# Graph layer with scattered messages: layer 2 one step after layer 1, the last group's layer 1 moved forward, and two half-size node blocks at the end

## The chip, the cores and the metric

The kernel runs on one core of a Trainium2 chip. The metric is device time in microseconds; for a set of runs the median is given, with the lowest and highest.

## What is computed

There are 12500 nodes with 64 features and 200000 edges, sorted by destination. Each edge takes its two nodes and its own 64 features, makes a message, and adds it to its destination. Then each node gets a small network on its sum, and a normalization. Cut to what matters:

```python
nodes = node_state[edges].reshape(num_edges, -1)            # rows src and dst, 128 features
gates = ssp(edge_state @ We1 + be1) @ We2 + be2             # ssp(x) = softplus(x) - log 2
gates = gates * (1.0 - sigmoid(5.0 * (edges_distance - 3.5)))
h = ssp(nodes @ Wn1 + bn1) @ Wn2 + bn2
messages = h * gates
message_sum = zeros_like(node_state).at[edges[:, 1]].add(messages)
new_state = node_state + (ssp(message_sum @ Ws1 + bs1) @ Ws2 + bs2)
out = layernorm(x + new_state)
```

All data is float32.

## The kernel before

**Groups.** The edges are cut into NG = 391 groups of 512, each in two halves of 256. Since they are sorted, the destinations of a half lie in a window of W = 42 nodes from a base that the kernel finds itself. The destination half of the first node layer is done once for all nodes at the start, into a table in memory (line 412); a group loads the 42 rows of its windows from it (`load`, line 143, with the edge features) and picks among them with a one-hot matrix.

**What one group does.** `gather` (line 135) fetches the 512 source rows by four indirect transfers from POOL, line 138. `onehot` (DVE, line 154) writes the window's one-hot columns beside them. `transposes` (PE, line 159) turn both into PSUM tile `tx`; `xcopy` (ACT, line 164) copies that to SBUF. `layer1_edge` (PE, lines 169 and 171) and `layer1_node` (PE, line 176) fill `z`. `exps` and `logs` (ACT, lines 183 and 186) and `softplus` (DVE, line 190) make `s`. `layer2_edge` (PE, lines 195 and 198) and `layer2_node` (PE, line 203) fill `gh`. `hcut` and `message` (DVE, lines 208 and 212) multiply the parts. `scatter` (PE, line 217) sums messages by window, and `window` (DVE, line 226) adds the windows into `sums`, which holds all nodes.

**Order.** The order is written out by hand in the loop of lines 435 to 468. Each engine works through its own instructions in that order. In step i, PE does layer 2's edge part of group i - 1, layer 1 of group i + 1, the transposes of i + 2, layer 2's node part of i - 1, and the scatter of i - 2. ACT does xcopy of i + 2 and then exp and log of i + 1. DVE does hcut and message of i - 1, window of i - 2, onehot of i + 4 and softplus of i + 1. SP issues the loads of group i + 5, POOL the gather of group i + 19; the first 20 gathers stand ahead of the loop. There are 24 gather buffers, two each of `z`, `gh`, `xT`, `u`, three of `s`, one of `tx` and `sc`.

**Node blocks.** A block is NB = 512 nodes in order; there are 25, the last with 212. Once every edge into a block is summed, `node_block` (line 228) does it in five parts, one per step: `hidden` (PE, line 247) and `clamp`; `logs` (ACT, lines 259 and 260) and `ssp` (DVE, line 263); `layer2` (PE, lines 268 and 271) and `center`; `square` and `variance`; `root` and `store`. PE's share goes between layer1_edge and layer1_node, into a free part of `z`; the rest goes at the end of the step. `clamp` loads y and `store` writes the result, both through SP's queue. `block_steps` (line 70) sets the step at which a block is put on the list, from the expected share of edges below its last node plus MARGIN = 3 steps. A guard (`least`, line 583, compared at line 373) makes the kernel redo what lies outside a window, or too early, in a second pass from line 477. Blocks that are left when the loop ends are done one part of each in turn, from line 469.

## Time and profile before

| what | value |
|---|---|
| median of 3 runs | 2621.21 us (2603.5 to 2627.03) |
| the profiled execution | 2002.57 us |
| its span, first to last instruction | 2000.7 us |
| PE busy | 1883.2 us, 94%, 11375 matmuls |
| POOL busy | 1487.4 us, 74% |
| DVE busy | 1119.8 us, 56% |
| ACT busy | 921.7 us, 46% |
| moved by DMA | 142.85 MB, 71 GB/s |

The profile is of one execution. Busy time is the time in which an engine ran an instruction; a share is of the span. A line number (L138) is that of the kernel above. A group of instructions is named by line, engine, operation and tiles (output <- input), with its count, busy time and the mean of one in ns. A wait is put down to the instruction or transfer that came last before the waiting one could start. PEclk is the granted clock of PE as a share of the full one. The timeline lists start and duration in us; an x4 after a row means that four such instructions were merged.

### The profile page before, as it was taken

The numbers are of one execution on the slowest core, as the hardware profiler recorded it, in microseconds if no ns is written. First come the engines' busy times: TensorE is split into PE (matmuls) and PEld (weight loads), VectorE is DVE, ScalarE is ACT, GpSimd is POOL, SyncE is SP. The second block draws the span as 40 slices with busy tenths as digits, with TensorE's granted clock in tenths as the row PEclk, the third lists the DMA queues.
The fourth block names the chain that finished last, engine by engine and source line by source line (L and its number), as shares of the span: only waits on it lengthen the run. The fifth ranks groups of instructions, "written<-read, shape, count | busy, mean of one in ns | idle before, by whom it ended". The sixth has DMA issues, their size and how long they took to land.

```text
span 2000.7 us, 37114 instructions
## 1 busy us (share of the span) xinstructions
PE 1883.2 (94%) x11375; PEld 1516.5 (76%) x11375; DVE 1119.8 (56%) x2762; ACT 921.7 (46%) x1315; POOL 1487.4 (74%) x1568
## 2 busy tenths in 40 slices
PE   4999999999999999999999999999999999999997
PEld 4788888888778777777877777777777777777775
DVE  4455555556546546554654655555465565665555
ACT  1355455454445444443544444444444454444443
POOL 7777777777777777777777777777777777777772
PEclk9999999999989999998999999999899999999997
DMA  8422222222222222222222222222222222222220
GB/s 235 137 79 66 66 68 67 67 69 63 69 62 62 68 61 68 65 65 58 72 57 75 64 58 72 71 64 61 58 71 71 67 67 68 64 67 71 71 71 22
DMA packets 168270, 142.85 MB, mean 71 GB/s; under 512 B 43599, under 2 KB 140027, under 8 KB 168066
## 3 DMA queue, kind: packets, MB, share of 16 engines
q1 hardware_dynamic: 116650, 87.54, 15.0%
q0 software_dynamic: 50048, 51.35, 11.5%
q10 hardware_dynamic: 1368, 1.51, 0.3%
q8 instruction: 95, 1.56, 0.3%
q14 instruction: 109, 0.89, 0.1%
HBM read 130.60 MB, written 9.63 MB: 70 GB/s over the span
## 4 chain that ended last, share of the span: by engine, by line
PE 59%; DMA 16%; POOL 12%; issue 7%; DVE 4%; DVEq 1%; ACT 0%; POOLq 0%; SPq 0%; ACTq 0%
DMA xg<-in_x,src_i 15%; POOL xg L138 12%; PE gh L203 11%; PE z L176 10%; PE gh L198 8%; PE z L171 8%; PE tx L159 6%; PE sc L217 6%; PE gh L195 4%; PE z L169 3%; PE z L412 2%; DVE s L190 1%; PE z L271 1%; PE z L247 1%; DVE h L208 1%
## 5 line engine op out<-in xcount | busy, mean ns | idle before, releaser
L138 POOL DMA_INDIRECT xg<-in_x,src_i x1564 | 1487.2, 951 | 479.1 <-issue 323.0
L164 ACT COPY xT<-tx 106x512 f32<-106x512 f32 x391 | 229.2, 586 | 982.4 <-PE tx L159 982.4
L208 DVE TENSOR_TENSOR h<-gh,cut 128x256 f32<-128x256 f32 x391 | 165.8, 424 | 586.6 <-PE gh L203 568.8
L176 PE MATMUL z<-xT,wns 106*128 106x256 f32 x1564 | 414.3, 387 | 0.1
L203 PE MATMUL gh<-consts,s 128*128 128x64 f32 x3128 | 396.2, 270 | 0.0
L203 PEld LDWEIGHTS gh<-consts,s 128*128 128x128 f32 x3128 | 391.4, 196 | 0.1
L190 DVE SCALAR_TENSOR_TENSOR s<-u,z 128x768 f32<-128x768 f32 x391 | 373.2, 955 | 23.5 <-PE z L176 8.1
L186 ACT ACTIVATE u<-u,one 128x768 f32<-128x768 f32 x391 | 365.7, 935 | 12.6
L176 PEld LDWEIGHTS z<-xT,wns 106*128 106x128 f32 x1564 | 301.9, 194 | 44.5 <-issue 0.8
L159 PE MATMUL tx<-consts,xg 128*106 128x128 f32 x1564 | 274.6, 282 | 52.5 <-DMA xg<-in_x,src_i 46.9
L183 ACT ACTIVATE u<-z 128x768 f32<-128x768 f32 x391 | 319.1, 816 | 1.4 <-PE z L176 1.4
L159 PEld LDWEIGHTS tx<-consts,xg 128*106 128x106 f32 x1564 | 196.4, 133 | 137.2 <-DMA xg<-in_x,src_i 86.2
L198 PE MATMUL gh<-consts,s 128*128 128x128 f32 x1564 | 280.8, 302 | 0.0
L171 PE MATMUL z<-eT,consts 128*128 128x256 f32 x782 | 278.0, 438 | 0.5 <-DMA eT<-in_eT 0.5
L198 PEld LDWEIGHTS gh<-consts,s 128*128 128x128 f32 x1564 | 205.7, 191 | 89.2 <-DVE h L208 81.3
L226 DVE TENSOR_TENSOR sums<-sums,sc 64x42 f32 x782 | 153.7, 197 | 185.9 <-issue 148.0
L217 PE MATMUL sc<-xg,msg 128*128 128x84 f32 x1564 | 246.4, 280 | 1.3 <-DVE sums L226 1.2
L217 PEld LDWEIGHTS sc<-xg,msg 128*128 128x128 f32 x1564 | 207.4, 193 | 1.5 <-issue 1.4
L212 DVE TENSOR_TENSOR msg<-gh,h 128x256 f32<-128x256 f32 x391 | 165.9, 424 | 13.4
L171 PEld LDWEIGHTS z<-eT,consts 128*128 128x128 f32 x782 | 118.1, 190 | 48.3 <-issue 1.6
L195 PE MATMUL gh<-row,ones 3*128 3x512 bf16 x391 | 151.1, 386 | 0.0
L154 DVE TENSOR_TENSOR xg<-consts,rel 128x168 f32<-128x168 f32 x391 | 130.6, 335 | 14.7 <-issue 2.8
(73 smaller groups left out, 562.9 us busy)
## 6 DMA issues: line engine op xcount, KB each, us to landing
eT<-in_eT SPq DMA_DIRECT2D x391, 128.0 KB
xg<-in_x,src_i POOLq DMA_INDIRECT x1564
wns<-table SPq DMA_DIRECT2D x782, 21.0 KB
table<-tb SPq DMA_DIRECT2D x14, 448.0 KB
sums<-in_xT SPq DMA_DIRECT2D x7, 455.0 KB
y<-in_x SPq DMA_DIRECT2D x24, 128.0 KB
out<-y SPq DMA_DIRECT2D x24, 128.0 KB
dst_h<-in_dst_h SPq DMA_DIRECT2D x1, 896.0 KB
```

The lines of the kernel that those rows point to most:

```text
L138: nc.gpsimd.indirect_dma_start(out=xg[:, k, :D], out_offset=None, in_=x, in_offset=bass.IndirectOffsetOnAxis(ap=src_i[:, g, k : k + 1], ax ...
L159: nc.tensor.transpose(tx[:, k, :], xgs[g][:, k, :DW], ident)
L164: nc.scalar.copy(xT, xTs[g])
L171: nc.tensor.matmul(zs[g][:, 0, :HE], we1.rearrange("a h d -> a (h d)"), eTs[g], start=False, stop=True, skip_group_check=True)
L176: nc.tensor.matmul(zn, wns[:, g % REST, h, :], xTs[g][:, h], start=True, stop=True, skip_group_check=True)
L183: nc.scalar.activation(us[g], z_of(g), AF.Exp)
L186: nc.scalar.activation(us[g], us[g], AF.Ln, bias=one)
L190: nc.vector.scalar_tensor_tensor(ss[g].rearrange("p i t e -> p (i t e)"), us[g], BIG, z_of(g), OP.min, OP.max)
L195: nc.tensor.matmul(gh, ones3[:, :P], row3.rearrange("q i k d -> q (i k d)"), start=True, stop=False, skip_group_check=True)
L198: nc.tensor.matmul(v[:, 0, t], ss[g][:, 0, t, :], we2, start=False, stop=False, skip_group_check=True)
L203: nc.tensor.matmul(ghs[g][:, 1, 2 * t + h, :], ss[g][:, 1 + h, t, :], wn2, start=False, stop=h == 1 and t == 1, skip_group_check=True)
L217: nc.tensor.matmul(sc, msgs[g][:, 2 * t : 2 * t + 2, :].rearrange("p h f -> p (h f)"), xgs[g][:, 2 * t : 2 * t + 2, D:DW], start=t == 0, s ...
```

## The change

The steps run from -2 to 391 and not from -4 to 392, and layer 2 of group i, not i - 1, is done in step i, the scatter of group i - 1, not i - 2. PE's order in a step is now layer 1 of i + 1, transposes of i + 2, layer 2 of i, scatter of i - 1. On ACT, exp and log of i + 1 precede xcopy of i + 2; on DVE, softplus of i + 1 precedes hcut. In step 388 the last group's layer 1 is placed among layer 2 of group 388, and its exp, log and softplus are done in two pieces, the edge part and the node part. Three loads and two onehots stand ahead of the loop.

The node blocks are now 26: 212 nodes, 23 of 512, and two of 256. The step of each is the expected share plus five standard deviations of the count of edges below its end. By that rule they are put on the list at steps 53, 96, 125 and so on to 384 and 388, and the last one after the loop; before, at steps 83, 115, 141 to 383, 391 and 394, the last two after the loop. From step 388 on a block's part uses a `z` tile of its own and stands at the end of the step. `center` and `store` have one DVE instruction less each, and `clamp` makes both its results from PSUM.

```diff
--- before.py
+++ after.py
@@ -60,16 +60,30 @@
 K = 4
 AHEAD = 20
 LOADS = 5
-MARGIN = 3
+SPREADS = 5
 CUTOFF = 5.0
 EPS = 1e-5
 LN2 = 0.6931471805599453
 BIG = 30.0
+def node_blocks(N):
+
+    rest = N - NB
+    first = rest % NB
+    assert rest > 0 and first % 2 == 0 and first <= HE
+    sizes = ([first] if first else []) + [NB] * (rest // NB) + [HE, HE]
+    return [(sum(sizes[:i]), n) for i, n in enumerate(sizes)]
+
+
 def block_steps(N, NG):
-    return [ceil(NG * sqrt(min(1.0, (b + 1) * NB / N))) + MARGIN for b in range(-(-N // NB))]
+    steps = []
+    for at, n in node_blocks(N):
+        share = sqrt(min(1.0, (at + n) / N))
+        spread = sqrt(share * (1.0 - share) / (NG * GE))
+        steps.append(ceil(NG * (share + SPREADS * spread)))
+    return steps
 @with_exitstack
@@ -178,16 +192,21 @@
     def z_of(g):
         return zs[g].rearrange("p b e -> p (b e)")[:, : 3 * HE]
-    def exps(g):
-        us[g] = work.tile([P, 3 * HE], F32, name="u")
-        nc.scalar.activation(us[g], z_of(g), AF.Exp)
-
-    def logs(g):
-        nc.scalar.activation(us[g], us[g], AF.Ln, bias=one)
-
-    def softplus(g):
-        ss[g] = work.tile([P, 3, 2, P], F32, name="s", bufs=3)
-        nc.vector.scalar_tensor_tensor(ss[g].rearrange("p i t e -> p (i t e)"), us[g], BIG, z_of(g), OP.min, OP.max)
+    every, edge, node = slice(0, 3 * HE), slice(0, HE), slice(HE, 3 * HE)
+
+    def exps(g, part=every):
+        if part.start == 0:
+            us[g] = work.tile([P, 3 * HE], F32, name="u")
+        nc.scalar.activation(us[g][:, part], z_of(g)[:, part], AF.Exp)
+
+    def logs(g, part=every):
+        nc.scalar.activation(us[g][:, part], us[g][:, part], AF.Ln, bias=one)
+
+    def softplus(g, part=every):
+        if part.start == 0:
+            ss[g] = work.tile([P, 3, 2, P], F32, name="s", bufs=3)
+        nc.vector.scalar_tensor_tensor(ss[g].rearrange("p i t e -> p (i t e)")[:, part], us[g][:, part], BIG,
+                                       z_of(g)[:, part], OP.min, OP.max)
     def layer2_edge(g):
         gh = gh_tile()
@@ -225,15 +244,13 @@
             part = sums[h * D : (h + 1) * D, bass.ds(base, W)]
             nc.vector.tensor_add(part, part, scs[g][h * D : (h + 1) * D, h * W : (h + 1) * W])
-    def node_block(b, pool):
-
-
-        left = N - b * NB
-        nq = min(2, -(-left // HE))
-        p = min(P, left // 2)
-        assert left >= NB or (nq == 1 and left % 2 == 0)
+    def node_block(first, n, pool):
+
+
+        nq = -(-n // HE)
+        p = min(P, n // 2)
         t = {}
-        rows = slice(b * NB, b * NB + nq * p * 2)
+        rows = slice(first, first + n)
         def tile3(name):
             return pool.tile([P, 2, 2, D], F32, name=name, bufs=2)[:p, :nq]
@@ -243,17 +260,17 @@
         def hidden(z):
             t["z"] = z[:, 1, HE:]
-            for q in range(2):
+            for q in range(nq):
                 nc.tensor.matmul(t["z"], ws1[:, q].rearrange("f o d -> f (o d)"),
-                                 sums[:, b * NB + q * HE : b * NB + (q + 1) * HE], start=q == 0, stop=q == 1,
+                                 sums[:, first + q * HE : first + (q + 1) * HE], start=q == 0, stop=q == nq - 1,
                                  skip_group_check=True)
         def clamp():
             t["y"] = tile3("y")
             nc.sync.dma_start(t["y"], x[rows, :].rearrange("(q p k) d -> p q k d", q=nq, k=2))
             t["l"], t["zb"] = (pool.tile([P, HE], F32, name=name, bufs=2) for name in ("l_s", "zb"))
+            nc.vector.tensor_scalar(t["l"], t["z"], packed["bs1"], BIG, OP.add, OP.min)
             nc.vector.tensor_scalar(t["zb"], t["z"], packed["bs1"], None, OP.add)
-            nc.vector.tensor_scalar(t["l"], t["zb"], BIG, None, OP.min)
         def logs():
             nc.scalar.activation(t["l"], t["l"], AF.Exp)
@@ -275,8 +292,7 @@
             nc.vector.scalar_tensor_tensor(t["y"], t["y"], 2.0, t["u"][:, :nq], OP.mult, OP.add)
             mean = small("mean")
             nc.vector.tensor_reduce(mean, t["y"], AX.X, OP.add)
-            nc.vector.tensor_scalar(mean, mean, 1.0 / D, None, OP.mult)
-            nc.vector.tensor_sub(t["y"], t["y"], mean.to_broadcast([p, nq, 2, D]))
+            nc.vector.scalar_tensor_tensor(t["y"], mean.to_broadcast([p, nq, 2, D]), -1.0 / D, t["y"], OP.mult, OP.add)
         def square():
             t["y2"] = tile3("y2")
@@ -296,9 +312,8 @@
             v, r = t["v"], t["r"]
             nc.vector.tensor_mul(v, v, r)
-            nc.vector.tensor_mul(v, v, r)
-            nc.vector.tensor_scalar(v, v, -0.5, 1.5, OP.mult, OP.add)
-            nc.vector.tensor_mul(r, r, v)
+            nc.vector.scalar_tensor_tensor(v, v, -0.5, r, OP.mult, OP.mult)
+            nc.vector.scalar_tensor_tensor(r, v, 1.5, r, OP.add, OP.mult)
             nc.vector.tensor_mul(t["y"], t["y"], r.to_broadcast([p, nq, 2, D]))
             nc.sync.dma_start(out[rows, :].rearrange("(q p k) d -> p q k d", q=nq, k=2), t["y"])
@@ -430,43 +445,69 @@
         with tc.tile_pool(name="finish", bufs=1) as finish:
-            steps = block_steps(N, NG)
+            blocks = list(zip(node_blocks(N), block_steps(N, NG)))
+            last = NG - 1
             todo = []
-            for i in range(-4, NG + 2):
-                def at(f, g, *more):
-                    if 0 <= g < NG:
-                        f(g, *more)
-                part = todo.pop(0) if todo and i + 1 < NG else None
-                if i == -4:
-                    for g in range(LOADS - 4):
-                        load(g)
+
+            def at(f, g, *more):
+                if 0 <= g < NG:
+                    f(g, *more)
+
+            for g in range(LOADS - 2):
+                load(g)
+            for g in range(2):
+                onehot(g)
+            for i in range(-2, NG + 1):
+                part = todo.pop(0) if todo else None
                 at(load, i + LOADS)
                 if i > 0:
                     at(gather, i + AHEAD - 1)
-                at(layer2_edge, i - 1)
-                at(layer1_edge, i + 1)
-                if part and part[0]:
-                    part[0](zs[i + 1])
-                at(layer1_node, i + 1, 0)
-                at(layer1_node, i + 1, 1)
+                ending = i + 2 >= last
+                if i < last - 1:
+                    at(layer1_edge, i + 1)
+                    if part and part[0] and not ending:
+                        part[0](zs[i + 1])
+                    at(layer1_node, i + 1, 0)
+                    at(layer1_node, i + 1, 1)
                 at(transposes, i + 2)
-                at(layer2_node, i - 1, 0)
-                at(layer2_node, i - 1, 1)
-                at(scatter, i - 2)
-                at(xcopy, i + 2)
-                at(exps, i + 1)
-                at(logs, i + 1)
-                at(hcut, i - 1)
-                at(message, i - 1)
-                at(window, i - 2)
+                if i + 2 == last:
+                    exps(last - 1)
+                    xcopy(last)
+                    layer1_edge(last)
+                at(layer2_edge, i)
+                if i + 2 == last:
+                    layer1_node(last, 0)
+                    layer1_node(last, 1)
+                at(layer2_node, i, 0)
+                at(layer2_node, i, 1)
+                at(scatter, i - 1)
+                if i + 2 == last:
+                    logs(last - 1)
+                    for some in (edge, node):
+                        exps(last, some)
+                        logs(last, some)
+                elif i + 1 < last:
+                    at(exps, i + 1)
+                    at(logs, i + 1)
+                    at(xcopy, i + 2)
+                if i + 1 < last:
+                    at(softplus, i + 1)
+                at(hcut, i)
+                at(message, i)
+                at(window, i - 1)
                 at(onehot, i + 4)
-                at(softplus, i + 1)
+                if i + 2 == last:
+                    softplus(last, edge)
+                    softplus(last, node)
                 if part:
-                    part[1]()
-                for b, step in enumerate(steps):
-                    if step == i:
-                        todo += node_block(b, finish)
-            for parts in zip_longest(todo, *[node_block(b, finish) for b, step in enumerate(steps) if step > NG + 1]):
+                    if ending:
+                        node_part(part)
+                    else:
+                        part[1]()
+                for block, step in blocks:
+                    if step == i and i < last:
+                        todo += node_block(*block, finish)
+            for parts in zip_longest(todo, *[node_block(*block, finish) for block, step in blocks if step >= last]):
                 for part in parts:
                     if part:
                         node_part(part)
...
-        for b in range(NBL):
-            for part in node_block(b, o):
+        for block in node_blocks(N):
+            for part in node_block(*block, o):
                 node_part(part)
...
-    for b, step in enumerate(steps):
-        least[2 * (step - 1) : 2 * NG] = (b + 1) * NB
+    for (at, n), step in zip(node_blocks(N), steps):
+        least[2 * step : 2 * NG] = at + n
```

## The prediction

> **What bounds the kernel now.** I read the page first, then the instructions of the gather's line, the table of waits, engine busy time in windows, and last the timeline of a middle step, of a step with a node block, and of the end.
>
> The page gives PE 94% busy and POOL 74%, which points at PE. The instructions of line 138 and the windows say otherwise.
>
> ```profile
> L138 POOL DMA_INDIRECT xg<-in_x,src_i x1564: 940/945/2280, 3.3 to 1965.7; - x196
> 200.00:300.00 100.00, 100.00 (x639) 82.68 (x637) 57.35 (x136) 50.49 (x69) 75.76 (x80) 1.00 0.26 67
> 1000.00:1200.00 200.00, 189.98 (x1147) 152.44 (x1146) 112.83 (x282) 93.42 (x135) 151.31 (x159) 0.97 0.25 63
> 1800.00:1950.00 150.00, 141.67 (x871) 112.92 (x871) 86.96 (x222) 70.95 (x105) 113.43 (x121) 1.00 0.27 72
> ```
>
> In the windows the columns are length, then busy time (count) of PE, weight loads, DVE, ACT, POOL, then the clock. POOL issues 80 gathers in every 100 us from start to end: (1965.7 - 3.3) / 1563 = 1.255 us each, 5.0 us per group of four. Its "idle" 0.30 us after each one never shrinks, so POOL has no room. PE is full at 200 us and no longer at 1000 us. The starts of line 169 in the timeline are 4.41 us apart where PE is not held up; so PE, which starts at 74 us with 15 groups gathered, catches up near 525 us, and from there has 5.0 - 4.41 = 0.59 us of room per step. The waits agree:
>
> ```profile
> PEld tx L159 <- DMA xg<-in_x,src_i: 86.2, 155, 1.7
> PE tx L159 <- DMA xg<-in_x,src_i: 46.9, 99, 1.4
> PE z L271 <- DVE l_s L263: 24.8, 24, 1.1
> ```
>
> The first two are PE standing at the transposes until the gather has landed. The third is another wait: a node block's second layer (line 271) stands for DVE's `ssp`, 1.03 us each time. The timeline of such a step, and a full-clock row of an ordinary step:
>
> ```profile
> 1000.53 1.03 PE L176 MATMUL z<-xT,wns 106*128 106x256 f32 x4
> ...
> 1957.28 0.42 DVE L263 SCALAR_TENSOR_TENSOR l_s<-zb,l_s 128x256 f32<-128x256 f32 x1
> 1957.75 0.80 PE L271 MATMUL z<-consts,l_s 128*128 128x128 f32 x4 [1.03 <-DVE l_s L263]
> 1958.35 1.92 PE L176 MATMUL z<-xT,wns 106*128 106x256 f32 x4
> ```
>
> After the wait the same four matmuls take 1.92 in place of 1.03 us: the clock has fallen to half. That step lasts 8.05 us; without the fall, 6.4. The end:
>
> ```profile
> 1965.74 0.94 POOL L138 DMA_INDIRECT xg<-in_x,src_i  x1 [0.30 <-issue]
> 1969.66 0.60 PE L159 MATMUL tx<-consts,xg 128*106 128x128 f32 x4
> 1982.72 0.20 DVE L226 TENSOR_TENSOR sums<-sums,sc 64x42 f32 x1 [0.34 <-DVE sums L226]
> 1982.98 3.78 PE L247 MATMUL z<-sums,consts 128*128 128x256 f32 x8 [0.82 <-DVE sums L226]
> 1994.85 0.29 DVE L302 TENSOR_TENSOR y<-y,rstd 106x128 f32<-106x128 f32 x1
> ```
>
> So the span is: POOL to 1966.7, then a tail of 34.0 us, of which 12.7 from the end of the last transposes (1970.27) to the last window sum (1982.92), and 17.8 for two node blocks after that, the last 5.5 being the store's transfer.
>
> **What the Trainium skill says.** "Perfetto Trace Analysis", section "GPSIMD Engine Instruction", says that a GpSimd span is unreliable and start-to-start spacing should be used; that is why I price a gather at 1.255 and not at the row's 951 ns. The same page, "DMA Instruction — SWDGE (GPSIMD)", says the instruction's end is not the landing: here PE is released 2.35 us after the start of a gather that takes 0.94. "TensorE: Matmul & The Clock Gate", "What's actually happening", says the clock halves after an idle window of about 3.4 us; this trace differs in part: nine stretches at 0.5 (six of 3.4 us, three of 13.7) come between 100 and 1975 us, each just after a wait of about one microsecond, not after a whole idle window.
>
> **The change part by part.**
>
> *Gathers.* Same 1564, same order, same first start. A gather waits for a buffer whose last reader, the scatter 24 groups back, now comes a step earlier; POOL shows no wait on it now. Cost 0, and POOL still ends at 1966.7.
>
> *Layer 2 one step after layer 1.* A step has the same matmuls: 0 for PE. Is the result of DVE ready? From the start of line 169: layer 1 done at 1.77, `exps` 0.82 and `logs` 0.94 to 3.6, `softplus` 0.95 to 4.6; layer 2 wants it at 4.41 + 1.61 + 0.44 = 6.46. It has 1.9 us to spare. `xcopy`, now behind `logs` on ACT, ends near 4.15; layer 1's node half wants it at 5.25: 1.1 to spare. If that cover went, PE would wait per step, but first out of its 0.59. Cost 0. The loads on SP keep their order and their distance of four steps; SP has 26 pairs of y and out transfers in place of 25, and an out that waits for DVE holds up only loads that are needed four steps (20 us) later. Cost 0.
>
> *Node block inside the steps.* Line 271 now comes after layer1_edge alone, no longer after layer2_edge too, 0.96 us earlier. DVE's order becomes softplus, hcut, message, window, onehot, ssp: hcut starts at 4.52 where a step takes 4.41 (softplus holds DVE) and at 4.65 where a late gather makes it 5.0; then 0.47 + 0.51 + 0.55 + 0.24 + 0.37 to ssp's start and 0.42 to its end, against line 271 at 1.12 in the next step. The wait becomes 1.15 to 1.6 us in place of 1.03: +0.1 to +0.6 each, 3 to 14 us of PE in 24 blocks. Behind the waiting matmul stand layer 1's node half, the transposes and layer 2, and ACT's exp waits for those. Cover: PE's 0.59 us per step. At the late spacing of 8 steps that is 4.7 us per block, against 0.86 (hidden layer: 5.27 - 4.41) + 0.95 (layer 2) + 1.6 = 3.4. So 0 on the path, unless half clock adds 1.65 (short stretch) or some 6 (long): that is the rival below. Fewer small DVE operations (one in center, one in store, 0.17 each) fall inside DVE's idle time: 0.
>
> *The end.* Block 384's layer 2 now comes in step 387, one step before the last transposes. Gather 390 lands at 1965.74 + 2.35 = 1968.1. PE's delay from the block, 0.86 + 2.55 less the room of three steps, leaves the last transposes ending at about 1970.0 with full clock, 1971.8 with half; 9 of 25 blocks went to half before; with a longer wait I take one in two: 1970.9, 0.6 later than now.
> From there to the last window sum, by PE's and DVE's queues: ACT does exp 389, xcopy 390 (to +1.1), log 389 (+2.05), the edge part's exp and log (401 and 508 ns by rows of 256 elements, lines 259 and 260; for 512 I take 613 and 707, an estimate by "ScalarE: Activation LUTs", "What ACT_TABLE_LOAD costs": 186 or 280 ns + 0.833 per element; its price for 768, 826 and 920, stands beside 816 and 935 here). PE: layer 1 edge, layer 2 edge 388, layer 1 node to +2.7, then 388, 389, 390. DVE sets the end: softplus 389, hcut and message 388, window, the two parts of softplus 390 (to +6.5), variance of block 384, hcut/message/window 389, its store (to +9.9), hcut, message 390, window 389 (+11.5), clamp of the next block (+13.1), window 390 to +13.9. Now 12.7: a loss of 1.2, since the small node work stands ahead of the last window on DVE.
> After it: layer 2 of block 388 (+0.4 to 1.6), hidden of the last block (2.6), center of the first (2.75), clamp (3.75; log may start at 3.25), exp and log to 4.2, ssp 4.65, layer 2 6.0, center 7.1, square 7.45, variance 7.95, root 8.45, store 9.5, transfer 5.5: 15.0. Now 17.8: a gain of 2.8 from 256 nodes and one chain in place of two.
> Sum: +0.6 + 1.2 - 2.8 = -1.0 us. Span 2000.7 - 1.0 = 1999.7, and 1.9 us around it.
>
> The median shown is 2621.21, 618.6 above the profiled execution's 2002.57, and no view says where those runs spend it. If POOL is slower there (2621 / 1564 = 1.68 us per gather at most), or PE is, the steps still hold the same work. I carry the difference in us over: 2621.2 - 1.0 = 2620.2, rounded 2620.
>
> **Rivals.** *Slower: half clock after each block.* The clock fell after windows in which PE was about 30% idle; a wait of 1.6 us in 3.41 makes that 47%. It decides when a block costs PE more than 4.7 us (0.59 by 8 steps). With a long stretch at every block: 3.4 + 6.2 = 9.6, which exceeds the room from step 190 on: 17.8 blocks by 9.6 less 194 steps by 0.59 = 56 us; with half of them long, 20. So 2641 to 2677; over 1% above about half long. Against: only a third were long, and the six short ones cost 5.05, hardly over the room.
> *Faster: the waits for ssp go, and the unprofiled runs are PE's.* (2621 - 105) / 391 = 6.4 us per step would then be PE at a partly halved clock, and its waits would count: 24 by 1.03 and nine stretches by 3.2 = 54 us, 2567. For: softplus no longer stands between onehot and ssp. Against: the working above makes the wait longer.
> *The change fails its guard:* if edges reach a block after its step, line 477's second pass runs and doubles the time. The steps stand five standard deviations above the mean, so this is 1 in 100 at most.
>
> **How the numbers follow.** Forecast 0.78, with its own range 2604 to 2638, from the bounds above (-4 to +13) and the shown scatter of 2603.5 to 2627.03; slower rival 0.11 (2660), faster rival 0.10 (2567), guard 0.01. A measurement of this kernel tells no less than about 1% from no change. The range 2585 to 2650 leaves out the faster rival, most of the slower one and the guard, 0.2. Faster by over 1%: 0.10; within 1%: 0.79 (the forecast and the mildest slower cases); slower: 0.11.
>
> **What would show it.** Right: L138's spacing still 1.255 and its last start near 1965.7; L271's wait 1.15 to 1.6; line 169's interval still 4.41 early; from the last window sum to the end 15 us. Wrong: PE waiting on softplus or xT in ordinary steps; more than five long half-clock stretches; no waits for the gather left after 1000 us; a first or last gather at another time.

## The result, and the profile after

| | before | after |
|---|---|---|
| median, lowest and highest, 6 runs each | 2624.12 us (2603.5 to 2643.89) | 2798.94 us (2774.64 to 2817.86) |
| ratio, 95% interval | | 1.0667 [1.0618, 1.0717] |

The change makes the kernel 6.7% slower, 175 us; the forecast was 2620 us. One thing has to be known to read any number below: the kernel before took 2591 to 2654 us in most sets of runs, but 2000 to 2016 us in two sets, and its profile above is of the second kind; so every ratio is taken on one chip, in one set. I call the two kinds late and prompt chips, for a reason that the timeline will show. It need not be the chip itself: the chip numbered 2 was prompt in one set (2003 us) and late in a later one (2631 us, beside `rows_even`). The fair partner of the profile after, taken on a late chip, is a second profile of the kernel before from a late chip (2613.4 us). The pages' lines, after first:

```profile
span 2800.3 us, 37803 instructions
PE 2415.9 (86%) x11378; PEld 1882.4 (67%) x11378; DVE 1109.9 (40%) x2725; ACT 921.2 (33%) x1322; POOL 1480.7 (53%) x1568
PEclk9997886767877757776767877886787778677697
```

```profile
span 2613.4 us, 37114 instructions
PE 2248.5 (86%) x11375; PEld 1801.6 (69%) x11375; DVE 1120.4 (43%) x2762; ACT 920.9 (35%) x1315; POOL 1484.4 (57%) x1568
PEclk9997877887877778877788777788778887888898
```

PE has practically the same number of matmuls but is busy 167.4 us longer, of 186.9 that the span grew. Its clock is lower: in its trace and in all others here it is either full or half, and the mean is 0.769 after and 0.819 before. The other engines' busy times stand still. The gather's line of the kernel after:

```profile
L152 POOL DMA_INDIRECT xg<-in_x,src_i x1564: 938/944/1426, 3.2 to 2662.7; - x196
  PE sc L236: 458.3, 112
```

Its last start is 2662.7, not 1965.7, and POOL stands 458 us for the scatter (line 236, line 217 of before) that frees its buffers: POOL follows PE. On a late chip that is so before the change too: POOL stands 348.6 us for the scatter, and the last gather starts at 2491.0. The waits of PE, after and then before, both on late chips:

```profile
PE z L190 <- ACT xT L178: 144.8, 39, 6.2
PE z L288 <- DVE l_s L280: 42.4, 21, 3.5
PE z L264 <- DVE sums L245: 25.6, 14, 3.2
```

```profile
PE z L176 <- ACT xT L164: 143.0, 60, 4.3
PE z L271 <- DVE l_s L263: 28.4, 16, 3.0
PE z L247 <- DVE sums L226: 24.5, 8, 4.6
```

The three lines are the same three waits: layer 1 for the copy, a node block's layer 2 for `ssp`, a block's hidden layer for the window sums. None has grown by as much as 15 us. So the loss is not time in which PE waits, but time in which it works slowly. The windows of 800 us (columns as in the prediction), after and before, say so too: PE busy 722 and 713 us, but 3411 and 3583 matmuls, at a clock of 0.75 and 0.79.

```profile
200.00:1000.00 800.00, 721.53 (x3411) 560.46 (x3409) 313.10 (x755) 273.71 (x375) 460.17 (x488) 0.75 0.21 48
```

```profile
200.00:1000.00 800.00, 713.43 (x3583) 570.88 (x3582) 330.56 (x793) 288.45 (x394) 482.87 (x512) 0.79 0.21 51
```

Why "late": on these chips an engine often starts long after what it waits for. In the step shown, of the kernel after, exp of a group starts 4.4 us after the last matmul of its layer 1 (241.28 + 1.03), and layer 1 of the next group then stands 4.34 us for the copy behind it. Over the whole trace the distance is over 1 us for 75 of 392 exps. On a prompt chip the same distance, in the kernel `lag2` below, is 0.04 us in at least 90 of 100 steps (both worked out from the traces).

```profile
241.28 1.03 PE L190 MATMUL z<-xT,wns 106*128 106x256 f32 x4
246.69 0.81 ACT L200 ACTIVATE u<-z 128x768 f32<-128x768 f32 x1 [6.49 <-PE z L185]
249.56 0.58 ACT L178 COPY xT<-tx 106x512 f32<-106x512 f32 x1 [1.09 <-remote]
250.19 2.07 PE L190 MATMUL z<-xT,wns 106*128 106x256 f32 x4 [4.34 <-ACT xT L178]
```

After the wait the four matmuls take 2.07 us, so the clock is at half, as in the prediction's step of block 384; here it happens in ordinary steps. What makes the signals late is not shown by any run. The trace of the kernel after shows one thing: POOL's last gather ends at 2663.6 us, and of the 21 exps that start over 5 us later, 20 start 0.04 us after their matmul. The lateness ends where the gathers end, on a late chip too.

**One table for all runs.** From the traces' records of PE's instructions and of the granted clock I worked out, between 200 us and 160 us before the end: the time that PE is idle, the time at half clock, and the unbroken stretches at half clock, with their number and mean length. Ratios leave out runs over 1.5% above the fastest of their kernel, and the profiles of `lag`, `nodes` and `after_nog` are of such slower runs (2866, 2643 and 2072 us), so their last three columns may lean high. The first rows are from late chips.

| kernel | ratio to before [95%] | idle us | half clock us | stretches x mean us |
|---|---|---|---|---|
| before again | 0.9988 [0.9962, 1.0015] | 234 | 911 | 83 x 11.0 |
| **after** | 1.0667 [1.0618, 1.0717] | 240 | 1236 | 67 x 18.4 |
| after again | 1.0669 [1.0613, 1.0725] | 247 | 1311 | 67 x 19.6 |
| nodes | 1.0002 [0.9965, 1.0039] | 249 | 932 | 85 x 11.0 |
| lag | 1.0784 [1.0712, 1.0855] | 225 | 1440 | 67 x 21.5 |
| xfirst | 1.075 (two runs, no interval) | 262 | 1232 | 73 x 16.9 |
| after_late | 1.0958 [1.0881, 1.1035] | 227 | 1437 | 55 x 26.1 |
| lag2_pe | 1.0414 [1.0367, 1.0462] | 341 | 969 | 73 x 13.3 |
| after_fill | 1.0423 [1.0382, 1.0463] | 270 | 789 | 68 x 11.6 |
| **before_edge** | 1.0878 [1.0773, 1.0983] | 243 | 1376 | 72 x 19.1 |
| after_bias | 0.9946 [0.9921, 0.9972] | 421 | 679 | 95 x 7.2 |
| after_rows | 0.9849 [0.9781, 0.9917] | 524 | 604 | 102 x 5.9 |
| before_rows | 0.9597 [0.9527, 0.9667] | 424 | 666 | 89 x 7.5 |
| **rows_even** | 1.0079 [1.005, 1.0107] | 447 | 464 | 87 x 5.3 |
| *prompt chips:* lag3 | 1.0024 [1.0013, 1.0036] | 66 | 65 | 10 x 6.5 |
| lag2 | 1.0317 [1.0287, 1.0346] | 52 | 191 | 16 x 12.0 |
| before_nog | 0.9546 [0.95, 0.9593] | 21 | 27 | 5 x 5.5 |
| after_nog | 1.0013 [0.9978, 1.0048] | 50 | 222 | 19 x 11.7 |
| rows_xfirst | 1.0041 [1.0028, 1.0053] | 236 | 157 | 39 x 4.0 |

The idle time of before and after is the same, and so, nearly, is the number of times the clock falls. Each stretch lasts 18 to 20 us in place of 11. A step without waits takes 8.21 us at half clock and 4.41 at full, so the 325 us more at half clock cost about 150 us, or 163 if everything took exactly twice as long: most of the 175 us by which the median grew.

### The profile page after: what moved, and what is told of

Read it like the earlier page. It is cut to its first block, busy times and chain, and to the rows that moved or that the text cites. A ratio compares the mean times of both kernels' runs of the same rounds, so it can differ in the third digit from the quotient of the medians.

```text
span 2800.3 us, 37803 instructions
## 1 busy us (share of the span) xinstructions
PE 2415.9 (86%) x11378; PEld 1882.4 (67%) x11378; DVE 1109.9 (40%) x2725; ACT 921.2 (33%) x1322; POOL 1480.7 (53%) x1568
## 4 chain that ended last, share of the span: by engine, by line
PE 79%; another core or an unknown queue 8%; ACT 4%; issue 4%; DVE 3%; DVEq 0%; DMA 0%; ACTq 0%; SPq 0%
PE z L190 18%; PE gh L222 14%; PE z L185 10%; PE gh L217 10%; PE tx L173 9%; PE sc L236 8%; PE gh L214 5%; PE z L183 3%; ACT u L200 2%; PE z L264 1%; ACT xT L178 1%; ACT u L203 1%; PE z L288 1%; PE z L427 1%
## 5 line engine op out<-in xcount | busy, mean ns | idle before, releaser
L190 PE MATMUL z<-xT,wns 106*128 106x256 f32 x1564 | 577.1, 507 | 160.1 <-ACT xT L178 144.8
L190 PEld LDWEIGHTS z<-xT,wns 106*128 106x128 f32 x1564 | 393.4, 258 | 266.0 <-ACT xT L178 167.3
L222 PE MATMUL gh<-consts,s 128*128 128x64 f32 x3128 | 490.4, 312 | 0.0
L222 PEld LDWEIGHTS gh<-consts,s 128*128 128x128 f32 x3128 | 484.9, 236 | 0.2
L185 PE MATMUL z<-eT,consts 128*128 128x256 f32 x782 | 340.6, 524 | 0.3 <-DMA eT<-in_eT 0.3
L217 PE MATMUL gh<-consts,s 128*128 128x128 f32 x1564 | 340.5, 350 | 0.0
L217 PEld LDWEIGHTS gh<-consts,s 128*128 128x128 f32 x1564 | 253.3, 231 | 115.9 <-issue 106.0
L173 PE MATMUL tx<-consts,xg 128*106 128x128 f32 x1564 | 316.1, 339 | 2.7 <-DVE xg L168 2.7
L236 PE MATMUL sc<-xg,msg 128*128 128x84 f32 x1564 | 302.9, 326 | 15.7 <-PE gh L222 8.8
L173 PEld LDWEIGHTS tx<-consts,xg 128*106 128x106 f32 x1564 | 257.2, 170 | 82.1 <-issue 37.9
L236 PEld LDWEIGHTS sc<-xg,msg 128*128 128x128 f32 x1564 | 260.5, 236 | 19.6 <-PE gh L222 11.3
```

The costliest lines, as they stand in the source:

```text
L173: nc.tensor.transpose(tx[:, k, :], xgs[g][:, k, :DW], ident)
L185: nc.tensor.matmul(zs[g][:, 0, :HE], we1.rearrange("a h d -> a (h d)"), eTs[g], start=False, stop=True, skip_group_check=True)
L190: nc.tensor.matmul(zn, wns[:, g % REST, h, :], xTs[g][:, h], start=True, stop=True, skip_group_check=True)
L217: nc.tensor.matmul(v[:, 0, t], ss[g][:, 0, t, :], we2, start=False, stop=False, skip_group_check=True)
L222: nc.tensor.matmul(ghs[g][:, 1, 2 * t + h, :], ss[g][:, 1 + h, t, :], wn2, start=False, stop=h == 1 and t == 1, skip_group_check=True)
L236: nc.tensor.matmul(sc, msgs[g][:, 2 * t : 2 * t + 2, :].rearrange("p h f -> p (h f)"), xgs[g][:, 2 * t : 2 * t + 2, D:DW], start=t == 0, s ...
```

## The experiments

**Which part of the change?** First the kernel before once more, then its parts.

> The kernel before, unchanged, so that its profile can be taken in the condition in which its times were taken (the profile shown is of an execution of 2002.57 us, the times are 2603 to 2644). If the timed executions are held by signals that reach the waiting engine late, as in the profile of the changed kernel, this profile shows ACT starting exp some us after layer 1's last matmul, a mean clock near 0.8 and a span near 2620. If instead POOL is slower in them, the spacing of line 138 is near 1.65 us and PE waits for gathers. Ratio 1.00.

`nodes` has the order of before and the node blocks of after (their sizes, their steps, and the shorter `clamp`, `center` and `store`); `lag` is the reverse, before's node blocks in after's loop (the first lines of its edit):

```diff
-SPREADS = 5
+MARGIN = 3
```

> The order of steps of before, with the changed kernel's node blocks (26 blocks, the earlier steps, two of 256 nodes, shorter center and store). If the order is the cause: 2610 to 2630 us, ratio 0.995 to 1.005. If the longer wait for ssp and the half clock behind it are the cause: 2750 or more, ratio 1.05 or more.

> The changed kernel's order of steps (layer 2 one step behind, xcopy behind log, the last group's layer 1 moved), with the node blocks of before. If the order is the cause, nearly all of the loss is here: 2770 to 2810 us, ratio 1.05 to 1.07. If the node blocks are the cause, about 2620 to 2640, ratio 1.00 to 1.01.

Measured: `nodes` 1.0002, `lag` 1.0784, a little more than expected. The order is the whole loss, the node blocks are none of it. In `xfirst` the copy goes back ahead of exp on ACT:

```diff
+                    at(xcopy, i + 2)
                     at(exps, i + 1)
                     at(logs, i + 1)
-                    at(xcopy, i + 2)
```

> The changed kernel with xcopy ahead of exp and log on ACT, as before; all else as changed. If late signals hurt because xT is ready too late for the next step's layer 1 (145 us of waits of line 190 for xT in the changed kernel), this gives much of the loss back: 2680 to 2740. If the one-step lag of layer 2 itself is what hurts, it stays at 2780 to 2820.

Measured: 1.075, from 2807.44 and 2819.05 us against 2617.56. That is far from the 2680 to 2740 us hoped for: the place of the copy alone gives little or nothing back.

**Lag, gathers, or waits?** These four ran on a prompt chip. `lag2` puts layer 2, scatter and window of the kernel after back to two steps behind, in the changed order of each engine. The two `nog` kernels leave computation out: they gather only for the first 24 groups, and later groups use those rows again. `lag3` puts the kernel before one step further apart, with one buffer more of `s` and `xg`. The cores of `lag2` and of the `nog` kernels:

```diff
-                at(layer2_edge, i)
+                at(layer2_edge, i - 1)
...
-                at(scatter, i - 1)
+                at(scatter, i - 2)
```

```diff
+        if g >= AHEAD + 4:
+            xgs[g] = xgs[g - AHEAD - 4]
+            return
```

> The changed kernel with layer 2, hcut, message, scatter and window put back to two steps behind layer 1; xcopy stays behind log, softplus ahead of hcut, the last group's layer 1 and the node blocks as changed. If the one-step lag is what costs: 2610 to 2650 us, ratio 1.00 to 1.01. If the new order on ACT and DVE costs: 2770 to 2810.

> The kernel before with gathers for the first 24 groups alone: later groups use the rows of 24 groups earlier again, so the sums are of other rows. If the late signals come with POOL's gathers, line 169's interval is 4.41 us throughout after about 150 us, no half clock but after node blocks, and the time is 1850 to 1950 us. If the signals are late for another reason, it stays near 2600.

> The changed kernel with gathers for the first 24 groups alone, as in the one before it. If the loss comes only through the late signals that the gathers bring: within 1% of the other without gathers, 1850 to 1950 us. If the one-step lag costs by itself (waits in ordinary steps, half clock after node blocks), it is 5 to 8% above the other.

> The kernel before with layer 2, hcut, message, scatter and window three steps behind layer 1 in place of two (one s buffer and one gather buffer more, node blocks one step later). If distance between layer 1 and layer 2 is what lets PE go on while a signal is late: faster than before, 2500 to 2590 us. If two steps are enough and the rest is set by the gathers: 2610 to 2635.

Measured: `lag2` 1.0317, so a loss is there with the lag of before as well. Without the gathers, the ratios are 0.9546 for before and 1.0013 for after, which makes after 1.049 of its partner: a loss is there without gathers too, so it does not need them. `lag3` 1.0024: on a prompt chip more distance gains nothing; the gain that was expected of it was for a late one. How large the loss of the kernel after is on a prompt chip was not measured, so these runs do not yet say what share the lag has. PE's waits in `lag2`:

```profile
PE z L288 <- DVE l_s L280: 37.0, 25, 1.8
PE z L264 <- DVE sums L245: 25.2, 25, 2.1
```

25 waits of 1.5 us for `ssp`, where the prediction had 1.15 to 1.6, and 25 of 1.0 us of the hidden layer for the window sums, which the prediction did not have. My next theory was that these two waits, each followed by half clock, are the loss. `after_late` moves the node block's PE share to the end of PE's step, where both results are long done:

```diff
-                    if part and part[0] and not ending:
-                        part[0](zs[i + 1])
...
                 at(scatter, i - 1)
+                if part and part[0] and not ending:
+                    part[0](zs[i + 1])
```

`lag2_pe` is `lag2` with `layer2_edge` at the head of PE's step, as before. `after_fill` adds work, one f32 matmul of 256 columns per step into an unused part of `z`:

```diff
+                    elif i > 0:
+                        nc.tensor.matmul(zs[i + 1][:, 1, HE:], ident, eTs[i + 1], start=True, stop=True,
+                                         skip_group_check=True)
```

> The changed kernel unchanged, to stand beside the three others on one chip. In the runs so far its order cost 5.6 to 8% where the gathers and the engines' signals came late (before 2617 us) and, with layer 2 two steps behind or without the gathers, 3.2 to 5.6% where they were prompt (before 2003 us). Theory (TensorE at half clock after the new waits for the window sums and for ssp): 1.03 to 1.08 times before on either chip, mean clock 0.04 to 0.06 below before's. Rival (lag one costs only where signals are late): within 1% of before if before takes about 2003 us here.

> The changed kernel with the node block's TensorE share (hidden, and the node layer 2 two steps later) moved from behind layer1_edge to the end of TensorE's step, behind scatter. Both waits seen in the changed order (about 1 us on the window sums, 1.5 to 1.8 us on ssp, 25 of each) should go, since what they wait for is then done a good part of a step earlier. Theory that these waits, and the half clock that follows them, are the loss: no idle time over 0.3 us at hidden and node layer 2, time below 1.02 times before. Rival (the half clock comes from the start and from the waits of ordinary steps): the two waits go but the time stays within 1% of the changed kernel's.

> The changed kernel with layer 2 back to two steps behind and with layer2_edge at the head of TensorE's step as in the kernel before; ScalarE's order (copy last) and VectorE's (softplus first) stay as changed. With the copy of lag two alone (layer 2's edge part behind the transposes) it was 1.032 times before. Theory A (TensorE's order, which puts hidden first in the step with nothing ahead of it to cover its waits): layer2_edge covers 1.1 us of each wait, time 1.00 to 1.01 times before. Theory B (the order on ScalarE and VectorE, with the window sums later in VectorE's step): still 1.02 to 1.035 times before.

> The changed kernel with one extra matmul (128x256, f32) per step ahead of layer1_node, written into the half of the z tile that is unused in that step; steps with a node block's share have none. It adds work: about 0.54 us at full clock in some 340 steps, 184 us of TensorE time, to a step of 4.41 us. Theory (idle windows bring the half clock, and it is what costs): mean clock above 0.9 and, where the changed kernel takes about 2800 us, a time below 2700 us in spite of the added work; where it takes about 2080 us, 1970 to 2080 us. Rival (the clock is lost for another reason, or the loss is waiting): the added work is paid in full, 184 to 340 us more than the changed kernel beside it.

Measured, on a late chip: in `after_late` the two waits shrink from 56.6 and 45.9 us (after again) to 2.9 and 2.1, and the kernel is slower still, 1.0958 against 1.0669, with more half clock (1437 us against 1311). The theory fell, and its rival, which had the time unchanged, did not come true either. `after_fill` does more work and takes 81 us less than the kernel after beside it (2750.53 against 2831.65), with 789 us at half clock against 1311: the clock outweighs the added work. Its mean clock of 0.85 and its time fall short of the 0.9 and 2700 us expected. `lag2_pe` misses both of its numbers: half clock is near that of before (969 against 911 us), but PE stands 225 us at layer 1's node half for the copy, against 143 in before. So the order on PE lengthens the half clock, and the orders on ACT and DVE can cost something of their own. In the kernel after they do not show as waiting (240 us idle, 234 before), so the parts do not simply add up.

**Why does the full clock come back later?** Here a half-clock step of each order, after first:

```profile
1151.29 0.39 PE L183 MATMUL z<-ones,be 3*128 3x256 bf16 x1
1151.61 1.22 PE L185 MATMUL z<-eT,consts 128*128 128x256 f32 x2
1152.63 1.91 PE L190 MATMUL z<-xT,wns 106*128 106x256 f32 x4
1154.33 1.06 PE L173 MATMUL tx<-consts,xg 128*106 128x128 f32 x4
1155.33 0.60 PE L214 MATMUL gh<-row,ones 3*128 3x512 bf16 x1
1155.86 1.22 PE L217 MATMUL gh<-consts,s 128*128 128x128 f32 x4
1156.87 1.81 PE L222 MATMUL gh<-consts,s 128*128 128x64 f32 x8
1158.47 1.09 PE L236 MATMUL sc<-xg,msg 128*128 128x84 f32 x4
1159.50 0.39 PE L183 MATMUL z<-ones,be 3*128 3x256 bf16 x1
```

```profile
328.68 0.60 PE L195 MATMUL gh<-row,ones 3*128 3x512 bf16 x1
329.21 1.22 PE L198 MATMUL gh<-consts,s 128*128 128x128 f32 x4
330.37 0.39 PE L169 MATMUL z<-ones,be 3*128 3x256 bf16 x1
330.68 1.22 PE L171 MATMUL z<-eT,consts 128*128 128x256 f32 x2
331.70 1.91 PE L176 MATMUL z<-xT,wns 106*128 106x256 f32 x4
333.40 1.06 PE L159 MATMUL tx<-consts,xg 128*106 128x128 f32 x4
334.26 1.12 PE L203 MATMUL gh<-consts,s 128*128 128x64 f32 x8
```

A half-clock step lasts 8.21 us in both kernels and is full of work, with no wait at all; yet in the first the clock stays at half, step after step, and in the second it comes back within line 203. Clock changes come at multiples of 3.41 us: in the kernel after at 215.66, 229.31, 249.79 and 277.10 us, for instance, which is 4, 6 and 8 such windows apart. So I cut the traces into these windows, sorted those at half clock in which PE is fully busy by what lies in them, and asked whether full clock follows. With the changed PE order (after, after again, xfirst, lag, before_edge): of windows with neither a 3-row bias matmul (lines 183 and 214) nor a scatter, full clock follows 186 times of 186; of the others, 145 times of 1471. With the order before (before again, nodes): 147 of 170, and 10 of 250. (The counts move by some tens with how a matmul that only touches a window's edge is counted; the contrast stays.)

In the first step above the two bias matmuls stand 4.04 us apart, and what lies between them is 3.72 us on one side; a window of 3.41 rarely falls inside. The other side has the scatter. In the second the two bias matmuls stand only 1.69 us apart, and lines 171 to 203 run 4.5 us without a bias matmul or a scatter, though their end is at full clock already. Clean windows are 11% with the changed order and 40% with the order before. That they decide is so far a reading of traces. Three edits test the bias matmuls' part of it; none changes the scatter. They are these: `before_edge` moves `layer2_edge` in the kernel before behind the transposes and nothing else; `after_bias` moves only layer 2's bias matmul of the kernel after to the head of the step, ahead of layer 1's; the `rows` kernels pad the bias operands with zero rows from 3 to 128.

```diff
-                at(layer2_edge, i - 1)
...
                 at(transposes, i + 2)
+                at(layer2_edge, i - 1)
```

```diff
+                at(layer2_bias, i)
                 if i < last - 1:
                     at(layer1_edge, i + 1)
...
                 at(layer2_edge, i)
```

```diff
-    ones3 = const.tile([PIECES, HE], BF16, name="ones3")
-    be3 = const.tile([PIECES, 2, D], BF16, name="be3")
...
+    ones3 = const.tile([P, HE], BF16, name="ones3")
+    be3 = const.tile([P, 2, D], BF16, name="be3")
...
```

> The kernel before with one move: layer2_edge goes from the head of TensorE's step to behind the transposes. Layer 2 stays two steps behind, the orders on ScalarE and VectorE and the node blocks stay. Theory (the 3-row bias matmul of layer 2, now apart from the one of layer 1, leaves few 3.41 us windows free of both): half-clock stretches of 5.5 windows (about 18.7 us) in place of 3.2 (11 us), as many of them, idle time as before; where signals come late 1.04 to 1.08 times before, where they are prompt 1.00 to 1.02. Rival (the lag and the orders on the other engines cost it): within 1% of before, stretches of 11 us.

> The changed kernel with one move: layer 2's bias matmul (3x512, bf16) goes to the head of TensorE's step, right ahead of layer 1's bias matmul; all else, lag one too, stays. Theory (position of the 3-row matmuls): stretches fall from 5.5 windows to 2.1 on average (about 7 us), and the time to 0.95 to 1.02 times before where signals come late. Rival (lag one or the ScalarE and VectorE orders): 1.05 to 1.08 times before as with the changed kernel.

> The changed kernel with the bias matmuls' operands padded by zero rows from 3 to 128 (ones, be, row, rs): the same order, the same number of instructions and columns. Theory (a matmul of 3 rows hardly counts as work for the clock): each takes as long as before, 0.2 to 0.4 us, stretches fall to 1.6 windows on average (about 5.5 us), time 0.92 to 1.01 times before where signals come late. Rival (it is the place or the type bf16, not the 3 rows): stretches and time as in the changed kernel, 1.05 to 1.08.

> The kernel before with the same padding of the bias matmuls to 128 rows. Theory: stretches fall from 3.2 windows to about 1.6, half of the 911 us at half clock goes, time 0.92 to 0.98 times before where signals come late, within 0.5% where they are prompt. Rival: no change, within 0.5%.

Measured, on a late chip: all four on the theory's side. `before_edge` 1.0878, above the 1.04 to 1.08 expected, with idle time as before (243 us) and stretches of 19.1 us: one moved line, no change of lag, and the whole loss is there. `after_bias`, stretches of 7.2 us for the 7 expected, ratio 0.9946: one moved matmul, and the loss is gone. `after_rows`, 5.9 us for 5.5. With 128 rows, of the fully busy half-clock windows that hold a bias matmul 80 of 92 are followed by full clock. `before_rows`, stretches of 7.5 us, longer than the 5.5 expected, 666 us at half clock, where half of 911 was expected, and 0.9597 [0.9527, 0.9667]: faster than both kernels, and the best ratio among the kernels that compute everything.

The scatter matters as well, by the same traces. In `after_rows`, windows with a padded bias matmul and no scatter were followed by full clock 70 times of 70, those with both only 11 of 23; in the two kernels with the order before, windows with a scatter and no bias matmul 0 times of 62 (touches under 0.1 us left out). So padding mends the bias matmuls and leaves the scatter, whose part no run here tests by itself.

Three of these times mix in a second effect. A step at full clock, 4.41 us in both kernels, is 4.11 in `after_bias` and 3.81 in the `rows` kernels. The start of the matmul behind layer 2's bias shows where it comes from, in the kernel after (3 rows) and in `after_rows`:

```profile
1182.31 0.39 PE L214 MATMUL gh<-row,ones 3*128 3x512 bf16 x1
1182.62 0.71 PE L217 MATMUL gh<-consts,s 128*128 128x128 f32 x4
1183.17 1.00 PE L222 MATMUL gh<-consts,s 128*128 128x64 f32 x8
```

```profile
2104.09 0.38 PE L214 MATMUL gh<-row,ones 128*128 128x512 bf16 x1
2104.30 0.61 PE L217 MATMUL gh<-consts,s 128*128 128x128 f32 x4
2104.75 0.44 PE L222 MATMUL gh<-consts,s 128*128 128x64 f32 x3
```

Behind 3 rows the next matmul starts 0.31 us later, behind 128 rows 0.21; and from the four matmuls after it to the next ones it is 0.55 and 0.45 us. So `rows_even` gives the 0.6 us back as two f32 matmuls per step, of 256 and 104 columns, ahead of layer 1's node half:

```diff
+                        for n in (HE, 104):
+                            nc.tensor.matmul(zs[i + 1][:, 1, HE : HE + n], ident, eTs[i + 1][:, :n], start=True,
+                                             stop=True, skip_group_check=True)
```

> The changed kernel with bias operands padded to 128 rows, and two extra f32 matmuls (256 and 104 columns, 128 rows) per step ahead of layer1_node, written into the half of the z tile that is unused in that step; they take 0.43 and 0.17 us, so that a step at full clock has 4.4 us as in the changed kernel. Theory (the clock alone): where signals come late, stretches of two windows or less, under 800 us at half clock in place of 1236 to 1311, and 1.01 to 1.04 times before, against 1.067 for the changed kernel; where they are prompt, 1.00 to 1.015. Rival (the padded kernel gained from the shorter step only): 1.06 to 1.07 where signals come late, 1.03 or more where they are prompt.

Measured: 1.0079 [1.005, 1.0107], just under the 1.01 to 1.04 expected, with unhindered steps of 4.46 us at full clock and 464 us at half clock. The order is as changed, the step is no shorter, and 6.7% have become 0.8%. Half clock fell by 772 us against the kernel after, worth about 360 us by the same reckoning; 207 us of that PE now spends waiting (447 us idle, 240 in the kernel after). The two added matmuls are full work themselves and can help the clock, as in `after_fill`; but `after_fill`, with 3 rows, kept 789 us at half clock and 1.0423, and `after_rows` has 604 us without them. Last, `rows_xfirst` has the copy ahead of exp in `after_rows`:

> The changed kernel with bias operands padded to 128 rows and with the copy of the transposes ahead of exp and log on ScalarE, as in the kernel before. Theory (with the half clock mended, TensorE's wait for the copy, 312 us in the padded changed kernel, is what is left): that wait falls below 270 us and the time to 0.955 to 0.975 times before. Rival (lag one, the waits at the node blocks or VectorE's order keep it): 0.98 to 0.99, as with the copy last.

It ran on a prompt chip: 1.0041 there says nothing on the question, which needed a late one. What makes `after_rows` (0.985) slower than `before_rows` (0.960) stays open. It is waiting and not the clock: PE is idle 524 us in the one and 424 in the other, with less half clock in the slower one (604 and 666 us).

## Why the prediction was wrong

- *Layer 2 one step after layer 1, "a step has the same matmuls: 0 for PE".* **This step failed.** The matmuls are the same and at full clock the step is 4.41 us, as I said. But their order sets how soon PE gets its full clock back, and that was worth most of the loss: 1236 us at half clock against 911, 8.8% for the moved `layer2_edge` alone, and 0.8% left with the bias matmuls padded and the step as long as before. I had priced the number of matmuls and not their order.
- *"I carry the difference over", 618.6 us.* Wrong as well, and the reason why a PE cost could not be hidden. I took POOL, the bound in the profiled execution, for the bound of the timed runs. There POOL waits on PE, so there is no 0.59 us of room per step. The faster rival also took these runs for PE's, but expected a gain from shorter waits; I gave it 0.10.
- *softplus and the copy, 1.9 and 1.1 us to spare.* On a prompt chip no step waits for either, with lag one too (`after_nog`). On late chips that cover is too thin, but no thinner than before: 144.8 us at layer 1's node half, 143.0 before.
- *Node block, 1.15 to 1.6 us for* `ssp`*.* Measured 1.5 us in `lag2`, and 2.0 us (42.4 by 21) in the changed kernel on a late chip. The hidden layer's wait of 1.0 us was missed: I set line 264's place in PE's step against `ssp`, not against the window sums, now last in DVE's step. Of these waits none decides: `after_late` is without them and slower.
- *The end.* From the last window sum (2785.80) to the end are 14.5 us, for 15.0 predicted, so this part was right; it is too small to matter here.
- *A reading.* At 74 us 54 gathers had started, 13 groups and not 15. It changes nothing: PE first stands for a gather at 526 us, for 525 predicted.
- *The rival "half clock after each block".* Right in kind and sign, wrong in place: with the blocks of after alone, `nodes`, nothing is lost. I had listed "more than five long half-clock stretches" as a sign of error; there were 67 stretches of 18.4 us on average. But on a late chip the kernel before has 83 as well, of 11.0 us, so the sign that counts is their length.
- *The Trainium skill,* "TensorE: Matmul & The Clock Gate", section "What's actually happening": full clock after one busy window of some 3.4 us. The windows agree (3.41 us). But windows full of work were not enough: 1326 of 1471 with a 3-row matmul or a scatter in them were not followed by it.

Not measured: the changed kernel itself on a prompt chip. `lag2` (1.032) and the pair without gathers (1.049) only suggest a loss there too.

## What to carry to other kernels

Where PE drops to half clock now and then, reordering its instructions is not free, even with the same work, no new wait and engines with room to spare: look how long each half-clock stretch lasts and what fills it. Keep matmuls of few rows together, or pad them with zero rows, and see if stretches shorten. And before pricing anything at 0 as hidden, make sure that the profiled execution is like the timed runs: 2003 against 2621 us was the sign that another engine set the time.

## What the runs showed of the hardware

- A 3-row bf16 matmul hardly counts as work for the clock: with 3 rows, 30 of 276 fully busy half-clock windows that hold one were followed by full clock (after again); padded to 128 rows, 80 of 92. Without a scatter in the window it was 28 of 149 and 70 of 70 (touches under 0.1 us left out).
- A fully busy half-clock window with a scatter (84 columns) and no 3-row matmul was followed by full clock in none of 62 cases (before again, nodes). That the scatter is the reason is a reading of traces, not tested.
- A 3-row matmul delays what follows: padding the two to 128 rows shortened the step by 0.60 us, from 4.41 to 3.81, though more rows are loaded and streamed.
- The same kernel took about 2003 us in some sets of runs and 2620 in others. In the slower sets ACT's exp often started late, 4.4 us after its matmul in the step shown; after POOL's last gather it no longer did. The cause is open.
